# Loads at both ends of a four-layer graph network begun in another order, and single VectorE operations at the seams of layers 0 to 2 in another order

## The chip, the cores and the metric

One core of a Trainium2 chip runs the whole program in one launch. The time is device microseconds of that core, a median of three executions. The engines are TensorE (PE, with its weight loads as PEld), VectorE (DVE), ScalarE (ACT), GpSimd (POOL) and SyncE (SP), which issues nearly all DMAs.

## The reference

Everything is float32. There are 3327 nodes with 256 features; `adj` is a sparse symmetric 3327 x 3327 matrix with a full diagonal. Four layers are applied, each to a normalised and rectified copy of the nodes and added back to them:

```
h = relu(layernorm(x));  x = x + adj @ (h @ W0.T + b0)                                  # layer 0
h = relu(layernorm(x));  x = x + relu(new_adj @ (tanh(h @ Wp + bp) @ Wg) + bg)          # layer 1
      # new_adj = the 700 largest entries of each row of tanh(adj * adj), where adj > 0
h = relu(layernorm(x));  x = x + relu(dinv * (adj + I) @ (dinv * (h @ W2.T)))           # layer 2
h = relu(layernorm(x));                                                                # layer 3
   for n in 0, 1:
      A  = softmax(q k.T) cut to the entries that make 0.9 of each row, made to sum to 1
      Xf = R @ Xf;  Xa = A @ Xa;  Z += Xf @ U1[n].T + Xa @ U2[n].T
   x = x + layernorm(h + Z) * g + b
```

A row of `adj` has far fewer than 700 entries above zero, so in layer 1 the kernel counts the entries and keeps them all; code that would do it otherwise runs only if a count asks for it.

## The kernel before

The nodes make 26 tiles of 128 rows. Tile p and tile p + 13 form a pair p (13 pairs), so that `adj` falls into a 2 x 2 of 13 x 13 blocks, and a product with it is made by seven half-size products instead of eight (a scheme of Winograd's kind). For that, the blocks of the right-hand side are combined on VectorE (`combining_nodes`: L396 to L399, in chunks of blocks, into `ts`), and the slabs of `adj` too.

*Layers 0 to 2.* `Feed` brings the slabs: `load` (L565) issues the four slabs `a_a` of a chunk on SP (L576), `adding` (L594) makes the sums of them on VectorE (L608 to L611, in layer 2 after adding the identity on the diagonal blocks, L607), and `upto(n)` (L623) says which loads and sums are begun ahead of chunk n. A chunk is a stretch of the 13 blocks: in layer 0 (0 to 5, 5 to 9, 9 to 13), one pair at a time (`Product`, matmuls at L669); in layers 1 and 2 (0 to 3, 3 to 6, 6 to 9, 9 to 11, 11 to 13), two pairs at a time (`Double`, matmuls at L763). `count` (in `counter`, L868) notes the entries above zero of each slab (`pos`, L874 and L876); L891 takes the counts. `Double.result` (L773) takes the products out of PSUM: two copies on ScalarE, then five VectorE operations, L786 to L790. The doubles share one set of PSUM: products 1, 2, 5 and 4 of the next double need the copies out of the way, products 6, 3 and 7 (in TensorE's order 1, 2, 5, 4, 6, 3, 7) the operations up to L790.

*Layer 1* has a hidden product in front: for each pair, `hidden` (L499) adds a bias on VectorE (L504) and takes a tanh on ScalarE (L505), both on the 128 x 512 of tiles p and p + 13 of the right-hand side `rhs`. It runs in between the products of layer 0 that are still going on, and for the last pair, 12, at the start of layer 1. There the last two chunks of `ts` are combined inside `doubles` (L817, with the condition on `b`), after the third and the fourth `upto`.

*The order of the work.* TensorE's order is written out by hand everywhere. VectorE, SP and ScalarE follow the program's order only in `first_two_in`, the start of layer 0; elsewhere a scheduler orders them from the program's order, `tc.high_priority()` and `tc.issue_after(x)`, which puts what follows behind instruction x.

*The start.* `first_two` warms TensorE up with 15 matmuls of 128 x 128 of the identity (L958; float32, so two passes each), and 4 more behind the first `turn`. `first_two_in` (L963) issues on SP the nodes (L969, tile groups 0:1, 1:2, 2:4, 4:6, 6:9, 9:12, 12:13, each for both halves of the nodes) with the weights `w0s` (256 KB, L976) behind group 0:1. For each pair, `measure` takes mean and variance (L416, L417), `apply` normalises (L426, L433), `turn` transposes on TensorE (L445) with an eviction on ScalarE, and `plain` multiplies with `w0s` (L457).

*The end.* Layer 3's last two tiles, 25 and 12, come from the last `PropagatedPair`. After its second phase (slabs at L1414, products at L1539, `whole` with L1560 to L1566 on VectorE), `shares` loads rows of x3 and u (L1633, L1634), `finish3` and `finish_last` load z (L1642, L1675), all behind `pair.loaded`, the last slab's load. GpSimd adds u and y to z (L1644, L1645, L1676, L1677) and a bias to x3 (L1655, L1678), VectorE adds the product (L1647, L1684, L1686), makes a layer norm and adds x3 (to L1657 and L1692), and SP stores (L1665, L1693).

The lines that the change touches, and what calls them:

Of the kernel before, what the change touches and what calls it, by code (L numbers as in the profile page):

```python
# [16 lines left out]
AF = mybir.ActivationFunctionType  # L17
ALU = mybir.AluOpType
# [6 lines left out]
P = 128  # L25
# [31 lines left out]
def kernel(  # L57
# [255 lines left out]
    def layers_0_to_2(again):  # L313
# [123 lines left out]

        evicted, hold = [], []

# [23 lines left out]
        class Pair:  # L463
# [35 lines left out]
            def hidden(self):  # L499
                acc = project(self.xT, wps, self.name)  # L500
                rows = self.rhs.pair(self.p)
                by = bps.rearrange("p (i j f) -> p i j f", i=1, j=2).to_broadcast([P, 2, 2, P])
                with tc.high_priority():
                    nc.vector.tensor_tensor(rows, acc, by, ALU.add)  # L504
                    nc.scalar.activation(rows, rows, AF.Tanh)  # L505

# [48 lines left out]
        class Feed:  # L555
# [3 lines left out]
            def __init__(self, layer, order, load_x, change=None, count=None, keep=(), many=lambda p: 1):  # L559
                self.layer, self.order, self.load_x, self.many = layer, order, load_x, many  # L560
                self.change, self.count, self.keep, self.made = change, count, keep, []
                self.quads, self.ready, self.x2, self.done = {}, {}, {}, [0, 0]
                self.to_count = None

            def load(self, p, c):  # L565
# [8 lines left out]
                for i, j in QUADS:  # L574
# [9 lines left out]
                    q[i, j] = s  # L584
                if self.count:
                    if self.to_count is None:
                        self.count(p, c, q, many)
                    else:
                        self.to_count.append(functools.partial(self.count, p, c, q))
# [4 lines left out]
            def adding(self, p, c):  # L594
                many = self.many(p)
                a, b = cuts(many)[c]
                name = f"{tag}{self.layer}_{p}_{c}"
                q = self.quads.pop((p, c))
                s1, s2, s4 = (
                    raw.tile([P, 6, P], F32, tag=f"s{n}", name=f"s{n}_{name}", bufs=2)[:, : many * (b - a), :]  # L600
# [22 lines left out]
            def upto(self, n):  # L623
# [3 lines left out]
                if not n and self.layer:  # L627
                    turns = (self.load, 1), (self.add, 1), (self.load, 2), (self.add, 2), (self.load, 3)
                elif self.layer:
                    turns = (self.add, n + 2), (self.load, n + 3)  # L630
                else:
                    turns = (self.load, n + 3), (self.add, n + 2)
                for what, upto in turns:
                    k = what == self.add
                    while self.done[k] < min(upto, len(self.order)):
                        what(*self.order[self.done[k]])
                        self.done[k] += 1
                    if what == self.load:
                        self.store(n)
# [11 lines left out]
        class Product:  # L651
# [25 lines left out]
            def result(self, behind=None):  # L677
# [6 lines left out]
                with tc.high_priority():  # L684
# [10 lines left out]
                    nc.vector.tensor_tensor(four[:, 0, :], p1, p2, ALU.add)  # L695
                    nc.vector.tensor_tensor(four[:, 3, :], u[:, 0, :], b[:, 1, :], ALU.add)
                return y.rearrange("p i j f -> p i (j f)"), p3
# [36 lines left out]
        class Double:  # L734
# [36 lines left out]
            def result(self):  # L771
# [11 lines left out]
                with tc.high_priority():  # L783
# [5 lines left out]
                    nc.vector.tensor_tensor(y0[:, 1:2, :], y1[:, 1:2, :], one(3), ALU.add)  # L789
                    return nc.vector.tensor_tensor(y1, y1, both(one(7)), ALU.add)  # L790

# [11 lines left out]
        def doubles(layer, rhs, feed, w, finish, todo, at_first, places, pair_after, following=None, counted=None):  # L803
# [5 lines left out]
            for p in range(0, H, 2):  # L809
# [5 lines left out]
                for c, (a, b) in enumerate(cuts(prod.many)):  # L815
                    feed.upto(n)
                    if first and b > CUTS[2][0]:  # L817
                        combine_nodes(rhs, a, b)
                    for at in prod.steps(c, a, b):
# [5 lines left out]
                left = todo[len(places[prod.many - 1]) :] if p else []  # L825
                with tc.issue_after(prod.result().ins):
                    feed.upto(n)
# [91 lines left out]
        if not again:  # L919
# [33 lines left out]
            def first_two(product):  # L953
# [5 lines left out]

                warm_up(15)  # L960
                with tc.manual_schedule(engines=IN_FIRST_TWO):
                    return first_two_in(product, warm_up)

            def first_two_in(product, warm_up):
                for a, b in ((0, 1), (1, 2), (2, 4), (4, 6), (6, 9), (9, 12), (12, 13)):
                    for i in range(2):
# [5 lines left out]
                        else:  # L972
                            for r in LAST_ROWS:
                                nc.sync.dma_start(x0[r, a_, :], x[a_ * P + r.start : a_ * P + r.stop, :])
                    if a == 0:
                        nc.sync.dma_start(w0s, w0t.rearrange("(c p) e -> p c e", p=P))  # L976
# [22 lines left out]
                pairs[0].measure()  # L999
                for p in range(2):  # L1000
                    pairs[p + 1].measure()
                    pairs[p].apply()
                between = itertools.chain(add(), combining_nodes(rhs0, *CUTS[0]))
# [142 lines left out]
    def layer_3_in(again, tag, big, ep, w3, sm3, h3, kT0, ksum0, left):  # L1146
# [901 lines left out]
        with tc.manual_schedule(engines=PE_ALONE):  # L2048
# [31 lines left out]
            for i, m in enumerate(ORDER):  # L2080
# [34 lines left out]
                else:  # L2115
# [12 lines left out]
                    if not phase:  # L2128
                        pair.half()
                    else:  # L2130
                        both = pair.whole()
                        if pair.last:
                            with tc.issue_after(pair.loaded.ins):
                                x3s, us = shares(f"{p}", (1, m), (0, p))
                            finish3(m, ys.pop(m), both[:, 1, :], f"{m}", pair.loaded, (x3s[:, 1, :], us[:, 1, :]))()
                            finish_last(
                                p, ys.pop(p), both[:, 0, :], pair.accs[2][:, :P], f"{p}", pair.loaded,
                                x3s[:, 0, :], us[:, 0, :],
# [85 lines left out]
```

## Time and profile before

| what | value |
|---|---|
| median of 3 runs | 2466.09 us (2465.77 to 2466.48) |
| the profiled execution | 2464.7 us |
| its span, first to last instruction | 2462.9 us |
| mean granted TensorE clock | 0.998 |
| first matmul starts | 1.53 us |
| layer 1's first matmuls, layer 2's first matmuls | 329.99, 611.92 us |
| last matmul ends, last store issued, span ends | 2450.40, 2457.28, 2462.9 us |
| DVE busy in 320 to 365 us, 365 to 408, 705 to 750 | 44.09 of 45, 38.03 of 43, 29.02 of 45 us |

Two lists of the profile carry most of what follows. The list of waits says for how long an engine sat idle before an instruction of a line and which instruction ended that. The timeline gives for each group of like instructions the start, the duration, the engine, the line, and the tiles written and read, and in brackets the idle time just before. The matmuls overlap one another: their durations are longer than the distance between two, and a stall of the stream is better read from start to start.

### The profile page before, as it was taken

What the parts mean: (1) busy time and instruction counts of PE and PEld (TensorE: products, weight loads), DVE (VectorE), ACT (ScalarE), POOL (GpSimd) and SP (SyncE); (2) the same over time, 40 slices, a digit from 0 to 9 for tenths busy, and PEclk for the clock granted to TensorE, in tenths of its full rate; (3) what the DMA queues carried; (4) which work ended last, traced back from release to release, by engine and by line L of the source; (5) the groups of instructions that cost most, each with busy time, mean ns of one, the idle gap of its engine ahead of it and who ended that gap; (6) DMA issues with size and microseconds to landing.
All of it is one profiled execution on the core that took longest, in us unless ns stands there. A gap on an engine that the chain in (4) does not pass through costs nothing.

```text
span 2462.9 us, 41138 instructions
## 1 busy us (share of the span) xinstructions
PE 2443.5 (99%) x14483; PEld 2105.2 (85%) x14483; DVE 2078.8 (84%) x5312; ACT 1071.4 (44%) x2074; POOL 287.2 (12%) x462
## 2 busy tenths in 40 slices
PE   9999999999999999999999999999999999999997
PEld 8999988889888897777777777778888888888887
DVE  7877799898867768889788787995899999999995
ACT  3000034443011126666566565654655555555551
POOL 2000010000000000000000100000113222222232
PEclk9999999999999999999999999999999999999999
DMA  6788855566978666322332323234534434443343
GB/s 205 248 272 272 289 174 181 180 196 191 300 226 268 196 198 190 118 81 83 110 110 72 98 87 112 86 104 120 155 104 138 133 115 125 135 140 121 115 139 113
DMA packets 278674, 387.79 MB, mean 157 GB/s; under 512 B 24253, under 2 KB 216250, under 8 KB 278458
## 3 DMA queue, kind: packets, MB, share of 16 engines
q1 hardware_dynamic: 257322, 367.54, 48.3%
q10 hardware_dynamic: 21136, 17.52, 2.2%
q8 instruction: 116, 1.90, 0.3%
q14 instruction: 100, 0.82, 0.1%
HBM read 315.37 MB, written 67.89 MB: 156 GB/s over the span
## 4 chain that ended last, share of the span: by engine, by line
PE 94%; DVE 3%; DMA 1%; issue 1%; POOL 0%; SPq 0%; ACT 0%; POOLq 0%; DVEq 0%
PE a L234 24%; PE acc_a L763 18%; PE f0a L1480 11%; PE f1a L1539 10%; PE acc_a L669 10%; PE pl_a L1213 6%; PE pt_a L223 6%; PE u L1610 2%; PE u L1591 2%; PE out_a L797 2%; PE prj_a L457 2%; PE f L1381 1%; DVE a_a L906 1%; PE pt_a L445 1%; DMA a_a<-in_adj_t_dram 0%
## 5 line engine op out<-in xcount | busy, mean ns | idle before, releaser
L226 ACT COPY eT_a<-pt_a 128x512 f32<-128x512 f32 (+1 forms) x364 | 196.3, 554 | 372.0 <-PE pt_a L223 369.5
L234 PE MATMUL a<-h3a,eT_a 128*128 128x256 f32 x1352 | 320.3, 381 | 0.2 <-ACT eT_a L226 0.2
L234 PE MATMUL a<-vs,eT_a 128*128 128x256 f32 x1352 | 320.2, 381 | 0.2 <-ACT eT_a L226 0.2
L1300 DVE MAX8 cand_a<-w 128x8 f32<-128x128 f32 x1352 | 284.9, 278 | 4.1
L234 PEld LDWEIGHTS a<-h3a,eT_a 128*128 128x128 f32 x1352 | 246.5, 189 | 45.2 <-issue 10.0
L234 PEld LDWEIGHTS a<-vs,eT_a 128*128 128x128 f32 x1352 | 244.8, 190 | 30.3 <-ACT eT_a L226 0.7
L1296 DVE SCALAR_TENSOR_TENSOR w<-e_a,t_a 128x896 f32<-128x896 f32 x208 | 229.3, 1102 | 3.4
L1238 ACT ACTIVATE e_a<-pl_a 128x1024 f32<-128x1024 f32 x260 | 184.4, 728 | 36.7 <-PE pl_a L1213 36.7
L223 PE MATMUL pt_a<-ident,e_a 128*128 128x128 f32 x1352 | 198.3, 272 | 0.0
L1287 DVE SCALAR_TENSOR_TENSOR w<-e_a,t_a 128x3328 uint8<-128x3328 f32 x52 | 191.6, 3684 | 4.4
L223 PEld LDWEIGHTS pt_a<-ident,e_a 128*128 128x128 f32 x1352 | 166.5, 141 | 29.4
L1324 DVE SCALAR_TENSOR_TENSOR e_a<-e_a,all_least 128x3328 f32<-128x3328 f32 x50 | 184.5, 3690 | 1.8
L763 PE MATMUL acc_a<-s_a,tsa 128*128 128x256 f32 (+1 forms) x728 | 169.1, 364 | 2.7 <-DVE y_a L790 2.4
L763 PE MATMUL acc_a<-a_a,tsa 128*128 128x256 f32 (+1 forms) x728 | 169.4, 365 | 0.5 <-DVE tsa L399 0.5
L1480 PE MATMUL f0a<-slab3a_0a,tsa 128*128 128x256 f32 (+1 forms) x728 | 161.4, 367 | 0.0
L1271 ACT ACTIVATE junk_a<-e_a,t_a 128x3328 uint8<-128x3328 f32 x52 | 159.8, 3073 | 0.4
L763 PE MATMUL acc_a<-a_a,rhs 128*128 128x256 f32 (+1 forms) x728 | 158.6, 365 | 0.0
L908 ACT ACTIVATE a_a<-a_a 128x768 f32<-128x768 f32 (+2 forms) x132 | 97.3, 748 | 136.6 <-DVE a_a L906 98.2
L1276 ACT ACTIVATE junk_a<-e_a,t_a 128x3328 uint8<-128x3328 f32 x50 | 153.3, 3066 | 0.0
L1539 PE MATMUL f1a<-tsa,slab3a_1a 128*128 128x128 f32 x1248 | 148.1, 276 | 0.0
L763 PEld LDWEIGHTS acc_a<-s_a,tsa 128*128 128x128 f32 x728 | 130.5, 190 | 19.5 <-issue 2.5
L1539 PEld LDWEIGHTS f1a<-tsa,slab3a_1a 128*128 128x128 f32 x1248 | 144.0, 192 | 1.8
(284 smaller groups left out, 4316.9 us busy)
## 6 DMA issues: line engine op xcount, KB each, us to landing
a_a<-in_adj_t_dram SPq DMA_DIRECT2D x216, 256.0 KB, 3.4
a_a<-in_adj_t_dram SPq DMA_DIRECT2D x144, 384.0 KB, 4.1
slab3a_0a<-s_dram SPq DMA_DIRECT2D x95, 384.0 KB, 4.0
slab3a_0a<-in_adj_t_dram SPq DMA_DIRECT2D x65, 384.0 KB, 3.9
slab3a_1a<-s_dram SPq DMA_DIRECT2D x60, 384.0 KB, 4.0
a_a<-in_adj_t_dram SPq DMA_DIRECT2D x60, 320.0 KB, 4.4
slab3a_1a<-in_adj_t_dram SPq DMA_DIRECT2D x48, 384.0 KB, 4.0
s_dram<-s_a SPq DMA_DIRECT2D x45, 256.0 KB, 4.5
```

What stands on the lines that cost most here:

```text
L223: nc.tensor.transpose(pt[:, j, :], e[:, k * P : (k + 1) * P], ident)
L226: last_turned.append(nc.scalar.copy(eT[:, : len(blocks), :], pt[:, : len(blocks), :]))
L234: nc.tensor.matmul(acc[:, :width], ready[g][:, j, :], rhs[:, k, :], start=(k == 0), stop=(k == T - 1))
L669: nc.tensor.matmul(self.acc[:, g, at : at + wide], quads[n][:, k - CUTS[c][0], :], t, start=(k == 0 and n in (1, 4)), stop=(k == H - 1 and ...
L763: nc.tensor.matmul(self.acc[n], t, slab[:, :, k - cuts(self.many)[c][0], :], start=(k == 0 and n in (1, 5, 6, 7)), stop=(k == H - 1 and n ...
L1238: last_exp.append(nc.scalar.activation(dst, src, AF.Exp, accum_out=parts[:, c : c + 1]))
L1287: nc.vector.scalar_tensor_tensor(junk, e, t, e, ALU.is_lt, ALU.mult, accum_out=got)
L1296: nc.vector.scalar_tensor_tensor(w[:, : (b - a) * P], eg, t, eg, ALU.is_lt, ALU.mult, accum_out=below[:, g : g + 1])
L1300: nc.vector.max(cand[:, 8 * k : 8 * k + 8], w[:, (k - a) * P : (k - a + 1) * P])
L1324: nc.vector.scalar_tensor_tensor(e, e, least, e, ALU.is_ge, ALU.mult, accum_out=kept)
L1480: nc.tensor.matmul(self.acc[:, self.at[n]], right_half(h3, ts, n, k), self.block(phase, at), start=not at, stop=at == len(units) - 1, skip ...
L1539: nc.tensor.matmul(self.accs[bank][:, c * P : (c + 1) * P], self.block(phase, at)[:, 0, :], right_half(self.h, self.ts, n, k), start=start ...
```

## The change

- At the start, `w0s` is loaded behind the node tiles 2:4 instead of 0:1, and the first warm-up has 11 matmuls instead of 15. The loop around `measure` and `apply` is written out and gives the same order.
- In `hidden`, the last pair's bias and tanh are made in two halves (one for tile 12, one for tile 25).
- In `doubles`, the last two chunks of `ts` are combined one chunk earlier: blocks 9 to 11 before the products of chunk 2, blocks 11 to 13 before those of chunk 3.
- In layer 2 the counts of a chunk are made where its sums are made (`to_add`), and not where it is loaded. In layers 0 and 1 they stay.
- `summed_up` holds the last VectorE operation with which a product was taken out of PSUM (of `Product` or `Double`), and what follows a product is put behind it: at the start of layer 2 the loads and sums from the third of `turns` on; at the other doubles as before, by L790.
- At the end, `loaded` is kept from the last pair's first phase, so that the loads of x3, u and z stand behind the last slab of phase 0 instead of phase 1.

```diff
                         ALU.subtract, ALU.mult,
                     )
 
-        evicted, hold = [], []
+        evicted, hold, summed_up = [], [], []
 
         def turn_pair(src, func, pool, t, bufs, name):
 
...
                 rows = self.rhs.pair(self.p)
                 by = bps.rearrange("p (i j f) -> p i j f", i=1, j=2).to_broadcast([P, 2, 2, P])
                 with tc.high_priority():
-                    nc.vector.tensor_tensor(rows, acc, by, ALU.add)
-                    nc.scalar.activation(rows, rows, AF.Tanh)
+                    for i in (slice(0, 1), slice(1, 2)) if self.p == H - 1 else (slice(0, 2),):
+                        nc.vector.tensor_tensor(rows[:, i], acc[:, i], by[:, i], ALU.add)
+                        nc.scalar.activation(rows[:, i], rows[:, i], AF.Tanh)
 
             def hidden_turned(self):
                 acc = bank(f"hid_{self.name}")
...
                 self.layer, self.order, self.load_x, self.many = layer, order, load_x, many
                 self.change, self.count, self.keep, self.made = change, count, keep, []
                 self.quads, self.ready, self.x2, self.done = {}, {}, {}, [0, 0]
-                self.to_count = None
+                self.to_count, self.to_add = None, {}
 
             def load(self, p, c):
                 many = self.many(p)
...
                     if self.change:
                         self.change(s)
                     q[i, j] = s
-                if self.count:
+                if self.count and self.layer == 2:
+                    self.to_add[p, c] = functools.partial(self.count, p, c, q, many)
+                elif self.count:
                     if self.to_count is None:
                         self.count(p, c, q, many)
                     else:
...
                 a, b = cuts(many)[c]
                 name = f"{tag}{self.layer}_{p}_{c}"
                 q = self.quads.pop((p, c))
+                if (p, c) in self.to_add:
+                    self.to_add.pop((p, c))()
                 s1, s2, s4 = (
                     raw.tile([P, 6, P], F32, tag=f"s{n}", name=f"s{n}_{name}", bufs=2)[:, : many * (b - a), :]
                     for n in (1, 2, 4)
...
                 self.store(n - 1)
                 if not n and self.layer:
                     turns = (self.load, 1), (self.add, 1), (self.load, 2), (self.add, 2), (self.load, 3)
+                    for what, upto in turns[:2]:
+                        what(*self.order[0])
+                    self.done = [1, 1]
+                    with tc.issue_after(summed_up[-1].ins) if self.layer == 2 and summed_up else nullcontext():
+                        self.turns(n, turns[2:])
+                    return
                 elif self.layer:
                     turns = (self.add, n + 2), (self.load, n + 3)
                 else:
                     turns = (self.load, n + 3), (self.add, n + 2)
+                self.turns(n, turns)
+
+            def turns(self, n, turns):
                 for what, upto in turns:
                     k = what == self.add
                     while self.done[k] < min(upto, len(self.order)):
...
                     nc.vector.tensor_tensor(u[:, 0, :], u[:, 2, :], p5, ALU.add)
                     nc.vector.tensor_tensor(four[:, 1:3, :], u[:, :2, :], b[:, 2:4, :], ALU.add)
                     nc.vector.tensor_tensor(four[:, 0, :], p1, p2, ALU.add)
-                    nc.vector.tensor_tensor(four[:, 3, :], u[:, 0, :], b[:, 1, :], ALU.add)
+                    summed_up[:] = [nc.vector.tensor_tensor(four[:, 3, :], u[:, 0, :], b[:, 1, :], ALU.add)]
                 return y.rearrange("p i j f -> p i (j f)"), p3
 
 
...
                     nc.vector.tensor_tensor(y0[:, 1:2, :], y0[:, 1:2, :], one(6), ALU.add)
                     nc.vector.tensor_tensor(y1, y1, both(y0[:, 1:2, :]), ALU.add)
                     nc.vector.tensor_tensor(y0[:, 1:2, :], y1[:, 1:2, :], one(3), ALU.add)
-                    return nc.vector.tensor_tensor(y1, y1, both(one(7)), ALU.add)
+                    summed_up[:] = [nc.vector.tensor_tensor(y1, y1, both(one(7)), ALU.add)]
 
             def weighed(self, t):
 
...
                     hooks[88] = functools.partial(counted, p, prod.many)
                 for c, (a, b) in enumerate(cuts(prod.many)):
                     feed.upto(n)
-                    if first and b > CUTS[2][0]:
-                        combine_nodes(rhs, a, b)
+                    if first and c in (2, 3):
+                        combine_nodes(rhs, *CUTS_OF_DOUBLE[c + 1])
                     for at in prod.steps(c, a, b):
                         if at in hooks:
                             hooks[at]()
...
                     if prod.many == 1 and c and following:
                         combine_nodes(following, *CUTS[c - 1])
                 left = todo[len(places[prod.many - 1]) :] if p else []
-                with tc.issue_after(prod.result().ins):
+                prod.result()
+                with tc.issue_after(summed_up[-1].ins):
                     feed.upto(n)
                 pairs = []
 
...
                     for _ in range(n):
                         nc.tensor.matmul(busy[:, :P], ident, ident, start=True, stop=True)
 
-                warm_up(15)
+                warm_up(11)
                 with tc.manual_schedule(engines=IN_FIRST_TWO):
                     return first_two_in(product, warm_up)
 
...
                         else:
                             for r in LAST_ROWS:
                                 nc.sync.dma_start(x0[r, a_, :], x[a_ * P + r.start : a_ * P + r.stop, :])
-                    if a == 0:
+                    if a == 2:
                         nc.sync.dma_start(w0s, w0t.rearrange("(c p) e -> p c e", p=P))
                 feed.to_count = []
 
...
                     run(prods[p].steps(c, *CUTS[c]))
 
                 pairs[0].measure()
-                for p in range(2):
-                    pairs[p + 1].measure()
-                    pairs[p].apply()
+                pairs[1].measure()
+                pairs[0].apply()
+                pairs[2].measure()
+                pairs[1].apply()
                 between = itertools.chain(add(), combining_nodes(rhs0, *CUTS[0]))
                 for p in range(H):
                     pairs[p].turn()
...
                     run(pair.steps(phase), {k * units // T: v for k, v in plan.items()})
                     if not phase:
                         pair.half()
+                        loaded = pair.loaded
                     else:
                         both = pair.whole()
                         if pair.last:
-                            with tc.issue_after(pair.loaded.ins):
+                            with tc.issue_after(loaded.ins):
                                 x3s, us = shares(f"{p}", (1, m), (0, p))
-                            finish3(m, ys.pop(m), both[:, 1, :], f"{m}", pair.loaded, (x3s[:, 1, :], us[:, 1, :]))()
+                            finish3(m, ys.pop(m), both[:, 1, :], f"{m}", loaded, (x3s[:, 1, :], us[:, 1, :]))()
                             finish_last(
-                                p, ys.pop(p), both[:, 0, :], pair.accs[2][:, :P], f"{p}", pair.loaded,
+                                p, ys.pop(p), both[:, 0, :], pair.accs[2][:, :P], f"{p}", loaded,
                                 x3s[:, 0, :], us[:, 0, :],
                             )
                         else:
```

## The prediction

> **What bounds the kernel now.** I read the page's busy times and the summary of its chain of waits first: who sets the pace?
>
> ```profile
> PE 2443.5 (99%) x14483; PEld 2105.2 (85%) x14483; DVE 2078.8 (84%) x5312; ACT 1071.4 (44%) x2074; POOL 287.2 (12%) x462
> PE 94%; DVE 3%; DMA 1%; issue 1%; POOL 0%; SPq 0%; ACT 0%; POOLq 0%; DVEq 0%
> ```
>
> TensorE does, nearly alone. The change takes next to nothing from its stream, so it can only gain where that stream stands still, ahead of it, and behind it. The list of waits on TensorE says how much that is:
>
> ```profile
> PE acc_a L763 <- DVE y_a L790: 2.4, 2, 1.6
> PE busy L958 <- POOL ident masks.py:199: 1.5, 1, 1.5
> PE acc_a L763 <- ACT rhs L505: 1.0, 1, 1.0
> PE pt_a L445 <- DVE xn_a L433: 0.6, 2, 0.3
> PE acc_a L763 <- DVE tsa L399: 0.5, 1, 0.5
> ```
>
> Columns: total, times, longest. The first, third and fifth rows are the seams, and each lies on a line that the change touches. Then both ends, as the chain of waits gives them (start, length, what), first the beginning:
>
> ```profile
> 3.59 4.63 DMA rhs<-in_x_dram
> 8.24 0.44 DVE st_a L416
> 8.93 0.34 DVE xn_a L433
> 9.31 0.75 PE pt_a L445 x4
> 10.10 1.99 PE prj_a L457 x8
> ```
>
> The program waits for the seventh load (rows 2 to 4, second half, landed 8.22), normalises the first tile of pair 1 behind it, and transposes; from 10.10 on TensorE runs. And the end, VectorE's timeline around the idle time that GpSimd ends:
>
> ```profile
> 2448.57 0.42 DVE L1566 TENSOR_TENSOR xf_1a<-xf_1a,f1a 128x256 f32<-128x256 f32 x1
> 2452.41 0.48 DVE L1684 SCALAR_TENSOR_TENSOR z<-xf_1a,rinv,z 128x256 f32<-128x256 f32 x1 [3.42 <-POOL z L1677]
> ...
> 2453.95 0.32 DVE L1686 SCALAR_TENSOR_TENSOR z<-f1a,rinv,z 128x128 f32<-128x128 f32 x1
> ```
>
> **The start.** In SP's order `w0s` leaves third place for seventh; no other load changes its order. Each 2-tile load and `w0s` carry 256 KB. Of the chain's two last loads, the first landed at 7.48 and the second at 8.22, one such load apart. With `w0s` no longer ahead of them I take each to land one load earlier, the second at 7.48, and `w0s` at 8.22. The rest follows: VectorE's statistics, normalising and transpose take 8.24 to 10.10 as before, less 0.74; the product with `w0s` could start at 9.36, 1.1 after `w0s`. Gain 0.74. Bounds: by SP's issue alone the load moves by one issue (0.43 + 0.04 in the chain) = 0.47; by the spacing of the two loads before (6.25 to 7.48), 1.23. If instead `w0s` slipped a place further, to 9.59 where the (4:6) load landed, the product would start near 9.65: 0.45. VectorE's loads (4:6), at 8.86 and 9.59, are past `w0s` anyway and keep their place. Warm-up: eight passes fewer. Its matmuls stand 0.213 us apart until 5.53 and 0.112 after (the clock rises 4.0 us after the first), so it ends 8 x 0.112 = 0.9 before its 7.09, at 6.2, still 0.67 behind the rise; and the first transpose follows at once: at 7.34 before, it waited for an input that stood on VectorE behind the statistics of pair 1 (landed 6.25), whose load now lands by about 4.9, so that its input is there by 6.2. So it costs nothing; if the clock did not rise in time, the price is a window at half rate.
>
> A rule stands against this cut. The Trainium skill, "TensorE: Matmul & The Clock Gate", section "Part 1: The HAM clock gate (the "warmup" mystery)", has the clock released after a busy window of about 3.4 us that runs freely, so that the rise can fall later in another execution. By it another 3.4 us at half rate would lose an estimated 1.7 us, and the sum below would be some 7 instead of 8.7; the trace has only the one rise, at 5.53, and I go by that.
>
> **Layer 0 to 1.** Two stalls. At 357.39 TensorE waits for the tanh L505 (until 358.42) though it reads only blocks 19 to 21: the write goes over tiles 12 to 25 at once. In halves the ranges no longer touch, so this wait falls away. At 363.87 it waits for L399 of blocks 9 to 11, which now stand right behind the halves, ahead of most of the sums, and are done at about 359.6 (two halves from 356.96, 0.35 each, then L396 to L399 at 0.33 and one sum of 0.6), where TensorE needs them near 362.3. From start to start the stream lost 358.42 - 355.93 - 1.295 = 1.20 and 364.39 - 362.85 - 0.864 = 0.68 (1.295 and 0.864 being the usual six- and four-matmul groups): **1.88**. By idle time the two are 1.04 + 0.52. What is late next: VectorE issues one more operation pair (0.1 us) and TensorE is then 1.9 ahead of it; the sums of 9 to 11 come at about 363.1 with TensorE there at 364.0, and L790 at about 376.2 with the need near 377.5. VectorE is busy 38 of 43 us in layer 1, so it catches up. Lower bound: all but the first wait reappears, 1.2.
>
> **Layer 1 to 2.** L790 ends at 618.00 because two `pos` operations stand ahead of it; it releases 618.15. They go behind it, two `ts` operations (0.33 each) come between. It then ends at 617.03, and TensorE, issuing from 615.81 + 1.295 = 617.10, waits at most 0.1. From start to start: 618.15 - 617.10 = 1.05, less 0.01 to 0.1: **1.04**.
>
> **First seam inside layer 2.** VectorE idles until 747.39 for a slab (landed 747.37) that `pos` counts, and L786 to L790 (751.33 + 0.69) stand behind it; TensorE waits until 752.16. Their inputs are there at 745.4, so ahead of `pos` they end at about 746.8. Gain 752.16 - 749.15 - 1.295 = **1.72**. What goes behind: two `pos` per chunk, 2 x 0.87 = 1.74 (six by 0.69 to 0.96 in the rows of L876), now before the sums. The smallest slack of a sum's first use after 660 us was 7.5 (I took each use's start less the end of its writer); the sum of this seam comes earlier than before, at 749.6 instead of 751.93. Counts are used 14 us late. So moving them costs nothing at 7.5 of slack and starts to cost at 1.74. At the other doubles there was no stall, and no gain.
>
> **The end.** Six loads of 128 KB were issued from 2443.21 on, because they stood behind the last slab, whose buffer came free at 2442.84. They landed to 2449.71, GpSimd's four additions and two more followed one another (0.72 each) to 2452.38, and L1684 waited 3.42. Behind the last slab of the first phase they go out at about 2424 to 2430, between the slabs of the second phase. GpSimd is done by about 2442.8 (the last addition needs the attention product of 2441.47). On SP they put six issues of 0.43 us ahead of slabs, and in the DMA engines 768 KB (2.6 us at the 300 GB/s moved there): 2.6 against the 8 us between the landing of these slabs, by 2433, and their first use at 2441.3. L1684 then needs only its place behind L1563, 2448.57. L1566 at 2448.99, L1647 2449.45, L1649 2449.96, L1685 2450.30, L1651 2450.50, and L1686 at 2450.58 instead of 2453.95, where the last matmul (end 2450.40, plus 0.13) becomes the other limit. Gain **3.37**; bounds 2.5 (a wait at the last addition or slab of 0.9) and 3.5. The tail behind L1686 stays.
>
> **Sum.** 0.74 + 1.88 + 1.04 + 1.72 + 3.37 = 8.75, or 8.1 with the idle rows (4.0) for the seams; I take 8.7. The profiled span of 2462.9 (time 2464.7, 1.8 around it) becomes 2454.2 and its time 2456.0. The median of runs is 1.4 above that execution: 2466.09 - 8.7 = **2457.4**.
>
> **Rivals.**
>
> 1. *The seams form again.* VectorE was busy 44.09 of 45 us at 320 to 365; the stalls were its lateness, and would be due again one product further on (margins worked out above: 0.1, 0.9, 1.3). For it: those margins; against: only two halves of an operation are added, the rest is order. Only both ends gain: 2466.09 - 0.74 - 3.37 = 2462.0, no change within what can be told.
> 2. *The start gives nothing or loses.* `w0s` and the loads around it share the DMA engines and land together, late, or the clock rises late. Seams and end: 8.01 less nothing to 1.7: 2458.1 to 2459.8.
> 3. *Slower: counts in the way.* Two `pos` ahead of the sums on VectorE, 30 chunks in six doubles of layer 2. It decides when the slack of a sum falls under 1.74: at 0.87, say, 30 x 0.87 = 26.1 are lost and the time is 2466.09 - 8.7 + 26.1 = 2483.5. For it: the sums come later at every chunk. Against: 7.5 us, and VectorE is busy 29 of 45 us there.
> 4. *The change does not do what it says*: VectorE's scheduler undoes an order. The order of instructions shows each move as told, so it is left with 0.03 and 2466.
>
> **How the numbers follow.** Forecast 0.67, rival 1 0.11, rival 2 0.14, rival 3 0.05, rival 4 0.03. The forecast's own range is 2455.7 (start 1.23, end 3.5: a gain of 9.4, and 1 us for the scatter of medians) to 2459.1 (start 0.47, seams 4.0, end 2.5: 7.0). To hold eight in ten I add rival 2 and the half-formed cases of rival 1 (half of the seams: 2466.09 - 0.74 - 2.3 - 3.37 = 2459.7, with the lower bounds about 2461): 2455.3 to 2461.0. A measurement tells about 0.2%, 4.9 us, from no change. Faster by more: forecast, rival 2 = 0.81, with a piece of rival 1 0.82; within: 0.12; slower: 0.06 (rival 3 and small losses).
>
> **What would show it.** The list of waits without L790, L505 and L399 over 0.2; the second transpose at 8.6 and the first product at 9.4; the clock's rise still near 5.5; L1684 1.8 before the last matmul's end and not 2.0 after it, with no idle time that GpSimd ends; and the last store 3.5 after the last matmul instead of 6.9. Wrong would be: a new row of waits for s_a or a_a in L763 in layer 2, or slabs at L1539 waiting for DMA behind the six loads.

## The result and the profile after

| | before | after |
|---|---|---|
| median, 15 runs each | 2465.49 us (2463.41 to 2467.11) | 2459.62 us (2458.61 to 2461.90) |
| profiled span | 2462.9 us | 2458.1 us |
| last matmul ends | 2450.40 us | 2448.55 us |
| last matmul's end to the span's end | 12.5 us | 9.5 us |

The ratio is 0.9976 with a 95% interval of 0.9969 to 0.9983: 5.9 us faster (4.2 to 7.6 by the interval), where 8.7 had been forecast. The list of TensorE's waits in the changed kernel (who waited for whom: total us, times, longest us; the lines have moved, L790 is now L804, L785 L799, L696 L710, L505 L506):

```profile
PE acc_a L777 <- ACT y_a L799: 2.4, 3, 1.7
PE acc_a L777 <- DVE y_a L710: 1.9, 1, 1.9
PE busy L973 <- POOL ident masks.py:199: 1.5, 1, 1.5
PE pt_a L445 <- DVE xn_a L433: 1.0, 1, 1.0
```

The three rows that the prediction wanted gone are gone: nothing waits for L804, for the tanh or for L399. But two rows stand in their place that it did not have: 2.4 us for the copies L799 on ScalarE, and 1.9 us for L710, the last operation that takes layer 0's last product out (0.2 before). They add up to 4.3 us; the seams' waits had been 4.0. So the stalls were exchanged, not removed? The start of the same matmul in the two traces tells how much of each gain lasted (after less before):

| matmul near (after) | 300 | 336 | 358 | 363 | 374 | 461 | 547 | 618 | 751 | last ends |
|---|---|---|---|---|---|---|---|---|---|---|
| difference, us | -1.00 | +0.63 | -0.57 | -1.35 | +0.41 | +1.05 | +1.32 | +0.28 | -1.46 | -1.84 |

The start brings 1.00, lost again at 336. The first seam brings 2.0 between 336 and 363, and 374 takes 1.8 of it. Two more stalls follow in layer 1. Behind 547 us come the steps at 618 (1.04) and 751 (1.74), and 0.4 in small ones. The one at 751 is no gain of the change, as the last part of this section and e11 show.

The places of the two losses, as the timeline has them (start, length, engine, line, what; in brackets the idle time before and who ended it). Layer 0's end, first VectorE, then TensorE:

```profile
332.68 0.95 DVE L616 TENSOR_TENSOR s_a<-a_a,s_a 128x768 f32<-128x768 f32 x1
...
334.56 0.95 DVE L921 SCALAR_TENSOR_TENSOR a_a<-a_a 128x768 f32<-128x768 f32 x1
335.43 0.41 DVE L708 TENSOR_TENSOR y_a<-u_a,acc_a 128x256 f32<-128x256 f32 x1
335.76 0.28 DVE L710 TENSOR_TENSOR y_a<-u_a,acc_a 128x128 f32<-128x128 f32 x1
```

```profile
332.88 1.46 PE L777 MATMUL acc_a<-a_a,tsa 128*128 128x256 f32 x6
336.19 1.10 PE L777 MATMUL acc_a<-s_a,tsa 128*128 128x256 f32 x4 [1.85 <-DVE y_a L710]
```

VectorE has sums and filters of layer 1 ahead of L708 and L710, and no gap. TensorE came 1.0 earlier than before, VectorE 0.63 later: it had waited until 305.66 for a slab that it counts (304.92 before). The end of the first double in layer 1, ScalarE and then TensorE:

```profile
372.55 0.84 ACT L923 ACTIVATE a_a<-a_a 128x768 f32<-128x768 f32 x1 [1.76 <-DVE a_a L921]
373.29 1.05 ACT L799 COPY y_a<-acc_a 128x512 f32<-128x512 f32 x2
```

```profile
371.67 1.03 PE L777 MATMUL acc_a<-a_a,tsa 128*128 128x256 f32 x4
374.40 0.92 PE L777 MATMUL acc_a<-a_a,rhs 128*128 128x256 f32 x3 [1.71 <-ACT y_a L799]
```

ScalarE sits idle for 1.76 us for a filter of VectorE's (L921), because the tanh L923 of a slab that is used later stands ahead of the copies in its queue. The kernel before had the same order there (the tanh at 371.85, the copies from 372.60 on), but TensorE needed the copies no earlier than they came. TensorE's next double may not write that PSUM until the copies are done.

The seams further on. VectorE ahead of 750 us in the changed kernel:

```profile
747.63 0.29 DVE L612 TENSOR_TENSOR a_a<-a_a,ident 128x128 f32<-128x128 f32 x1 [1.49 <-DMA a_a<-in_adj_t_dram]
747.84 0.69 DVE L802 TENSOR_TENSOR y_a<-y_a,y_a 128x512 f32<-128x512 f32 x1
...
749.09 0.69 DVE L804 TENSOR_TENSOR y_a<-y_a,acc_a 128x512 f32<-128x512 f32 x1
749.69 0.95 DVE L891 SCALAR_TENSOR_TENSOR pos<-a_a,pos 128x768 bf16<-128x768 f32 x1
```

The counts are behind L804 now, but the addition of the identity, L612, is still ahead of it, and it waits for a slab of its own: that one landed at 747.60, the slab that the counts wait for at 745.15. So L804 ends at 749.8, in time, and not at 746.8. The kernel before has the same addition (L607 there) in the same place, and its slab landed at 749.78:

```profile
749.87 0.28 DVE L607 TENSOR_TENSOR a_a<-a_a,ident 128x128 f32<-128x128 f32 x1
...
751.33 0.69 DVE L790 TENSOR_TENSOR y_a<-y_a,acc_a 128x512 f32<-128x512 f32 x1
```

From the start of this addition to the end of the last sum it takes 2.14 to 2.15 us in both, and in every one of the fourteen profiles of this study, whether the counts are ahead or behind. Without the counts ahead of it, L790 would therefore have ended near 751.9 by this estimate, and it ended at 752.01.

And both ends. First TensorE at the beginning, then VectorE at the end:

```profile
8.31 0.75 PE L445 MATMUL pt_a<-ident,xn_a 128*128 128x128 f32 x4 [0.97 <-DVE xn_a L433]
9.13 1.97 PE L457 MATMUL prj_a<-w0s,xT_a 128*128 128x256 f32 x8
```

```profile
2446.79 0.48 DVE L1700 SCALAR_TENSOR_TENSOR z<-xf_1a,rinv,z 128x256 f32<-128x256 f32 x1
2447.20 0.41 DVE L1582 TENSOR_TENSOR xf_1a<-xf_1a,f1a 128x256 f32<-128x256 f32 x1
...
2448.85 0.32 DVE L1702 SCALAR_TENSOR_TENSOR z<-f1a,rinv,z 128x128 f32<-128x128 f32 x1
```

The first product starts 0.97 earlier. L1700 is ahead of the last matmul's end (2448.55) by 1.8, as foretold, and L1702 is 0.30 behind it, where it was 3.55.

### The profile page after: what moved, and what is told of

The parts are those of the page before. It is cut to its first block, busy times and chain, and to the rows that moved or that the text cites. A ratio compares the mean times of both kernels' runs of the same rounds, so it can differ in the third digit from the quotient of the medians.

```text
span 2458.1 us, 41131 instructions
## 1 busy us (share of the span) xinstructions
PE 2441.2 (99%) x14475; PEld 2103.9 (86%) x14475; DVE 2078.7 (85%) x5313; ACT 1070.9 (44%) x2075; POOL 292.9 (12%) x462
## 5 line engine op out<-in xcount | busy, mean ns | idle before, releaser
L923 ACT ACTIVATE a_a<-a_a 128x768 f32<-128x768 f32 (+2 forms) x132 | 97.4, 748 | 139.8 <-DVE a_a L921 98.0
L777 PEld LDWEIGHTS acc_a<-a_a,rhs 128*128 128x128 f32 x728 | 129.8, 190 | 19.4 <-ACT y_a L799 3.9
```

What stands on the lines that cost most here:

```text
L777: nc.tensor.matmul(self.acc[n], t, slab[:, :, k - cuts(self.many)[c][0], :], start=(k == 0 and n in (1, 5, 6, 7)), stop=(k == H - 1 and n ...
```

## The experiments

Every ratio below is to the kernel before, run on the same chip; the interval is 95%.

| run | median us (runs) | before | ratio (interval) |
|---|---|---|---|
| e1 changed kernel again | 2459.98 (10) | 2466.16 (32) | 0.9976 (0.9966 to 0.9985) |
| e2 start alone | 2464.73 (11) | 2466.16 | 0.9997 (0.9988 to 1.0006) |
| e3 end alone | 2463.44 (11) | 2466.16 | 0.9988 (0.9979 to 0.9997) |
| e4 seams alone | 2463.38 (11) | 2466.16 | 0.9991 (0.9982 to 1.0000) |
| e5 copies first | 2457.45 (5) | 2465.35 (15) | 0.9964 (0.9950 to 0.9978) |
| e6 fewer counts | 2457.24 (5) | 2465.35 | 0.9965 (0.9952 to 0.9979) |
| e7 slabs behind L710 | 2462.34 (11) | 2465.35 | 0.9988 (0.9978 to 0.9997) |
| e8 first seam undone | 2460.60 (11) | 2465.21 (17) | 0.9979 (0.9970 to 0.9988) |
| e9 e5, first seam undone | 2458.28 (7) | 2465.21 | 0.9970 (0.9959 to 0.9981) |
| e10 e5, late count | 2455.98 (5) | 2465.21 | 0.9961 (0.9947 to 0.9974) |

**e1, the changed kernel again.** No edit.

> The changed kernel once more, to see whether the two new waits come back. Theory A (VectorE works without a break from about 306 to 376 us, and the copies L799 on ScalarE stand behind a tanh that waits for it, so what TensorE wins ahead of 374 us is lost there again): waits on L710 near 1.9 us in all and on L799 near 2.4, 5 to 6 us faster than before. Rival B (one slab landed late by chance in that one profile): the wait on L710 at most 0.5 us, and the time 7 to 9 us faster than before.

L799 2.2 us in all, 1.7 of it at 373 us; L710 1.1. The wait on the copies belongs to the kernel. That on L710 came back smaller, between the two theories: part of it varies. There is also a wait of 0.5 us on L804, near 796 us: VectorE stood idle for 3.68 us until the slab of L612 had landed (792.96), and four of the five operations that take the product out stood behind it.

**e2, the start alone**, on the kernel before:

```diff
-                warm_up(15)
+                warm_up(11)
...
-                    if a == 0:
+                    if a == 2:
                         nc.sync.dma_start(w0s, w0t.rearrange("(c p) e -> p c e", p=P))
```

> Only the start of the change (w0s later, 11 warm-up matmuls) on the kernel before. Theory A: TensorE's first product starts 1.0 us earlier, but this is lost as a longer wait on L696 near 335 us (0.23 before, 0.8 to 1.2 then), so 0 to 0.4 us of gain in the time. Rival B: nothing takes it back, 0.9 to 1.0 us of gain.

The first product starts at 9.10, and at 335 us TensorE waits 0.79 for L696, about what theory A said; but other profiles with the old order have 0.2 to 1.3 there, so this one wait does not decide. The median is 1.4 us lower, but the interval has no change in it, so the time does not decide either. Nothing waits for L790 at 750 us in this profile.

**e3, the end alone**, on the kernel before:

```diff
                     if not phase:
                         pair.half()
+                        loaded = pair.loaded
...
-                            with tc.issue_after(pair.loaded.ins):
+                            with tc.issue_after(loaded.ins):
                                 x3s, us = shares(f"{p}", (1, m), (0, p))
```

and `loaded` for `pair.loaded` in the two calls that follow.

> Only the end of the change (x3, u and z loaded behind phase 0's last slab). Both theories: nothing before 2420 us moves; from the last matmul to the end 9.5 us instead of 12.5, so 3.0 us of gain. If it were 3.4, as forecast, the 0.3 us more that the last store took in the profile after would be chance.

2.7 us by the medians, and 10.1 us from the last matmul to the end in the profile. Over all profiles of this study that stretch is 12.1 to 13.1 us in the five with the old end (mean 12.5) and 9.4 to 10.1 in the nine with the new (mean 9.7): 2.8 us.

**e4, the seams alone**: the changed kernel with the edits of e2 and e3 undone, so

```diff
-                warm_up(11)
+                warm_up(15)
...
-                            with tc.issue_after(loaded.ins):
+                            with tc.issue_after(pair.loaded.ins):
```

> Only the order at the seams of layers 0 to 2, with start and end as before. Theory A: the waits on L505 and L399 go and come back as a wait of 1.4 to 1.8 us on the copies L799 near 373 us; what stays is the gain at 617 and 750 us, 2.6 to 3.2 us in all. Rival B: 4.2 to 4.7 us, with no new wait in layer 1 over 0.3 us.

2.8 us by the medians, 1.7 us of wait on L799, 1.6 on L710: as theory A had it, and not 4.6. That the sum agrees is partly luck: theory A counts 1.6 us at 750, which e11 and e12 show to be no gain, and the interval reaches from no change to 4.4 us. With the start as before, L710 is waited for 1.6 us all the same.

**e5, the copies first.** On the changed kernel; the tanh of the last two slabs of a double's second chunk waits for its place behind the copies:

```diff
-                        self.change(s)
+                        self.change(s, late=p and c == 1 and i)
...
                     for y, b in zip(self.ys, self.banks):
-                        nc.scalar.copy(y, b.rearrange("p (n f) -> p n f", n=2))
+                        copied = nc.scalar.copy(y, b.rearrange("p (n f) -> p n f", n=2))
+                with tc.issue_after(copied.ins):
+                    while late_tanhs:
+                        late = late_tanhs.pop(0)
+                        nc.scalar.activation(late, late, AF.Tanh)
...
+            if late:
+                late_tanhs.append(a)
+                return
             with tc.issue_after(evicted[-1].ins) if evicted else nullcontext():
                 nc.scalar.activation(a, a, AF.Tanh)
```

> The changed kernel, with one more order: in layer 1 the tanh of the last two slabs of each double's second chunk is begun behind the two copies L799 on ScalarE, not ahead of them. Theory A1 (what takes TensorE's gain back at 373 us and at the later ends of doubles is this place in ScalarE's queue): no wait on L799 over 0.3 us in layer 1, nothing in its place, so 1.5 to 2.5 us faster than the changed kernel (7.5 to 8.5 faster than before). Rival A2 (VectorE as a whole is late there, and the copies only show it): the wait comes back a few products later on L804 or on a sum, 0 to 0.7 us faster than the changed kernel.

ScalarE at the same place, and TensorE's list of waits, in e5:

```profile
370.63 0.84 ACT L931 ACTIVATE a_a<-a_a 128x768 f32<-128x768 f32 x1 [1.11 <-DVE a_a L926]
371.38 1.05 ACT L799 COPY y_a<-acc_a 128x512 f32<-128x512 f32 x2
373.15 0.84 ACT L803 ACTIVATE a_a<-a_a 128x768 f32<-128x768 f32 x1 [0.71 <-ACT y_a L799]
```

```profile
PE acc_a L777 <- DVE y_a L710: 2.0, 1, 2.0
PE busy L981 <- POOL ident masks.py:199: 1.5, 1, 1.5
```

The copies start right behind the matmuls that they read, the next double follows without a stall, and no other wait appears in layer 1. From the matmul near 336 us, which L710 releases, to the one near 374 it takes 36.34 us here and 38.21 in the changed kernel. The time is 7.9 us below the kernel before, as theory A1 had it: it was the place in ScalarE's queue. By the medians that is 1.7 to 2.0 us below the changed kernel, less than the intervals are wide, but four of the five runs lie below all 25 of the changed kernel (2457.91 at the least).

**e6, fewer counts.** The last pair is not counted in layer 0:

```diff
             def count(p, c, q, many=1):
+                if not i and p == H - 1:
+                    return
...
                 m = p + i * H
+                if not i and p == H - 1:
+                    nc.gpsimd.memset(counts[:, m : m + 1], 0.0)
+                    return
```

> The changed kernel without the counting of the last pair in layer 0 (left out: the nine counting operations of that pair on VectorE, about 5 us of its work near 290 to 309 us, and its column of counts is set to zero). Theory A (VectorE, busy without a break from 306 to 376 us, is late, and starts that stretch when a slab that it counts has landed): the wait on L710 falls below 0.3 us and the one on L799 at 373 us below 0.5, 2 to 3.5 us faster than the changed kernel. Rival B (the waits come from landings that do not depend on VectorE): both stay over 1 us.

```profile
PE acc_a L777 <- ACT y_a L799: 2.0, 4, 1.5
PE busy L978 <- POOL ident masks.py:199: 1.5, 1, 1.5
```

The wait on L710 is gone from the list: that one is VectorE's lateness. Without the counts VectorE has both less to do and one slab less to wait for; this run does not part the two. The copies are still waited for, 1.5 at 371 us: this half of theory A's expectation failed, since both engines came earlier and the order in the queue stayed. Time as much below before (8.1 us) as e5.

**e7, slabs behind L710.** On the changed kernel:

```diff
-                    with tc.issue_after(summed_up[-1].ins) if self.layer == 2 and summed_up else nullcontext():
+                    with tc.issue_after(summed_up[-1].ins) if summed_up else nullcontext():
```

> The changed kernel with layer 1's second chunk, loads, filters and sums, put behind the last operation that takes layer 0's last product out (L710): three filters of 0.87 us leave VectorE's queue ahead of L710, and four operations of the last blocks of ts (0.33 each) come in. Theory A (VectorE's amount of work, not its order, sets this stretch): the wait on L710 goes, but one of 1 to 2 us comes at the sums or filters of the second chunk near 341 us, and the time is within 1 us of the changed kernel or slower. Rival (order alone): no wait in its place, 1.1 to 1.9 us faster than the changed kernel.

```profile
PE acc_a L777 <- DVE s_a L613: 3.3, 1, 3.3
PE busy L973 <- POOL ident masks.py:199: 1.5, 1, 1.5
PE acc_a L777 <- ACT y_a L799: 1.0, 1, 1.0
```

L710 is off the list, and a wait of 3.3 us on the second chunk's sum is on it, ending at 343.6 us. VectorE's order only chooses what is late in this stretch. By the medians it is some 3 us slower than the changed kernel. The wait is longer than the 1 to 2 us that were expected, and in this profile the idle time also throttled the clock (last section).

**e8 and e9, the first seam undone**, in the changed kernel and in e5:

```diff
-                    for i in (slice(0, 1), slice(1, 2)) if self.p == H - 1 else (slice(0, 2),):
-                        nc.vector.tensor_tensor(rows[:, i], acc[:, i], by[:, i], ALU.add)
-                        nc.scalar.activation(rows[:, i], rows[:, i], AF.Tanh)
+                    nc.vector.tensor_tensor(rows, acc, by, ALU.add)
+                    nc.scalar.activation(rows, rows, AF.Tanh)
...
-                    if first and c in (2, 3):
-                        combine_nodes(rhs, *CUTS_OF_DOUBLE[c + 1])
+                    if first and b > CUTS[2][0]:
+                        combine_nodes(rhs, a, b)
```

> The changed kernel with the first seam as before: the last pair's bias and tanh in one piece, and the last two chunks of ts combined one chunk later. Theory A (TensorE's gain at this seam only waits longer for ScalarE's copies at 373 us): waits of 1.0 us on the tanh and 0.5 on L399 come back, the one of 1.7 us on the copies at 373 us falls below 0.3, and the time is within 0.7 us of the changed kernel. Rival (the gain of 1.9 us forecast for this seam is there): 1.5 to 2.0 us slower than the changed kernel.

> The kernel of e5 (copies ahead of the late tanhs), with the first seam as before, as in e8. Theory A: with the copies out of the way, the seam is worth what its waits were, so this one is 1.2 to 2.0 us slower than e5. Rival (VectorE's lateness takes the gain in any case): within 0.5 us of e5.

In both, the waits on the tanh (1.0) and on L399 (0.5) come back, and in e8 none is left at 373 us: the longest on the copies is now 0.9, at 548. By the medians below their own before, e8 stands at 4.6 us where the changed kernel has 5.9 to 6.2, and e9 at 6.9 where e5 has 7.9. By these the seam is worth 1.3 to 1.6 us in the changed kernel and 1.0 in e5, between the theories both times; but each of these differences is smaller than the intervals are wide. The traces say more. From the matmul near 336 us (released by L696 or L710) to the one near 374 it takes 38.43 us in all seven profiles with the first seam as before (before, e2, e3, e8, e9, e11, e12), 38.21 in the three with the new seam and ScalarE's queue as it was (after, e1, e4), and 36.34 and 36.27 with the copies first (e5, e10). Up to 374 us the seam is then worth 0.2 us in the changed kernel and 2.1 with the copies out of the way, close to theory A both times. What the medians show beyond that is not explained by this seam.

**e10, the copies first and a late count.** On e5, the last pair's upper half is counted in layer 2, where these slabs pass again:

```diff
+            def count2(p, c, q, many=1):
+                count2_(p, c, q, many)
+                if p == H - 1:
+                    count0(p, c, q, many)
```

with layer 0 leaving this pair out, and the counts of pairs 10 and 11 taken 16 steps earlier (`hooks[72 if p == 10 else 88]`), so that their tile comes free.

> The kernel of e5, with the counting of the last pair's upper half moved from layer 0 to layer 2, where that pair's slabs pass again (nothing is left out). Theory A: the wait on L710 near 335 us falls below 0.3, as in e6; 1.5 to 2.5 us faster than e5, less what eight more counting operations cost at the end of layer 2 (0 to 1.5 us as a wait on y near 905 us). Rival: VectorE's work at the end of layer 2 costs all of it, same as e5 or slower.

```profile
PE busy L989 <- POOL ident masks.py:199: 1.5, 1, 1.5
PE pt_a L445 <- DVE h3a L489: 1.0, 1, 1.0
PE pt_a L445 <- DVE xn_a L433: 0.5, 1, 0.5
```

Behind the start no wait over 0.1 us is left in layers 0 and 1; one of 1.0 came near 897 us, not on y but on a node tile that VectorE makes for layer 3. 9.2 us below before, and its five runs (2455.49 to 2457.17) lie below all 25 of the changed kernel (2457.91 at the least). By the medians it is the fastest kernel of this study, 1.3 to 1.5 us ahead of e5, where theory A less its costs had 0 to 2.5; the intervals of the two overlap.

**e11 and e12, the kernel before twice more**, for its waits (one run each, 2465.14 and 2467.00 us). No edit.

> The kernel before once more, unchanged, for its waits alone. Theory (the wait of 1.6 us on L790 at 750 us was one late landing, and so no part of what the change can gain): no wait over 0.2 us near 750 us, as in e2 and e3, which have the old order there; the one of 0.9 near 617 us is there again; near 335 us 0.2 to 0.8 us on L696. Rival (it belongs to the old order): 1.2 to 1.6 us near 750 us again.

> The same a third time, with the same expectations as e11; of the waits on the copies L785 at the ends of layer 1's doubles, between none and 3 us in all, as landings fall.

Two rows of e11's list:

```profile
PE acc_a L763 <- ACT y_a L785: 1.2, 2, 1.0
...
PE acc_a L763 <- DVE y_a L790: 0.9, 1, 0.9
```

In all four further profiles with the old order (e2, e3, e11, e12) the wait on L790 is 0.9 us, once, near 618 to 622; the 1.6 near 750 us is in none (0.05 at most). It is a race: in e11 the slab of L607 landed at 749.74, as late as in the first profile (749.78), but TensorE came there 2.4 us later and did not wait. The copies, absent from the list of the first profile, are waited for 0.4, 3.1, 1.2 and 1.9 us. And L696: 0.8, 0.5, 1.3, 1.3, against 0.2.

## Why the prediction was right, and where not

**The time** lay in the stated range, but the gain was only two thirds of the 8.7: less than the forecast's own range (7.0 to 9.4), and nearest to the half-formed case of rival 1 (2459.7, a gain of 6.4). There is luck in it: of the five terms, 1.7 us of the first seam came back as another wait, and the 1.72 at 750 us was no gain of the change.

**The start.** Forecast 0.74 at the first product; it was 0.97 between the two first profiles, and over all of them 10.1 to 10.6 us became 8.3 to 9.1 (means 10.27 of five, 8.81 of nine): 1.46. The mechanism was right and the term too small: 0.97 lies within its bounds, the mean beyond the upper one of 1.23. That it stays with the program was not shown: e2's interval includes no change, and its profile loses half of its 1.00 to L696 at 335 us. What releases TensorE there is tied to the count of one slab (next paragraph), which began at 305.8 us in the mean of the five profiles with the old start and at 305.2 in that of seven with the new one. Against 1.46 at the first product this is 0.6, within a scatter from 304.2 to 306.6: most of the start's gain is likely waited for at that place.

**Layer 0 to 1.** Here a step failed: "What is late next". It compared VectorE's sums and L790 with TensorE's need and found 0.9 and 1.3 us to spare. It left out that the next double also needs the copies on ScalarE, and that these stand behind a tanh whose input VectorE makes late. That queue gave up 1.7 of the 1.9 us ten microseconds on (waits of 1.71, 1.71 and 1.70 us in the first profile, e1 and e4), so that 0.2 of the 1.88 stayed. At later doubles it costs up to 0.7 us in these three, but 0 to 3.1 with the old order too. e5 shows the cause by taking it away. Rival 1 named the right weakness (VectorE's lateness) and the wrong engine for its place. And L696, 0.2 us in the profile at hand and so left alone, is 0.2 to 1.3 in five profiles with the old order and 1.1 to 2.0 in six with the new one (0 in e6, e7, e10). How late VectorE is there was decided by the count that begins when a slab has landed, at 304.2 to 306.6 us: L696 or L710 ends 30.4 to 30.6 us later in ten profiles of both orders (31.1 in e12, where another slab was late; e6 and e10 do not count it, and e7 has another order). Up to that count VectorE and SP have the same order in e4 as in the kernel before, so the order at the seams does not make these waits longer. With the old start the new order has 1.6 in e4, where that count began last of all, at 306.60; with the new start TensorE is there earlier and the slab hardly so.

**Layer 1 to 2.** Right, in place and size: 1.04 forecast, 1.04 measured, and the 0.9 us wait is in every profile with the old order. L804 ends at 618.25 and not at 617.03, because VectorE and TensorE were both 1.3 us later there.

**The seam inside layer 2.** Forecast 1.72, and the profile after shows 1.74: but the agreement is luck, and this was no gain of the change. No other profile of the old order has the stall. Two steps failed. A single wait for DMA was read as a fixed cost. And "ahead of `pos` they end at about 746.8" left out the addition of the identity (L607, now L612), which stands among these sums and waits for a slab of its own, landed at 749.78: with that slab, moving the counts would have freed L790 some 0.1 us earlier, by the 2.15 us that follow this addition in every profile. It kept its place, so such a stall can return, as in e1 near 796 us. Moving the counts cost nothing, as said: no wait for a sum in layer 2 appears, and rival 3 found no case.

**The end.** Mis-sized: 3.37 against 2.8 over all profiles (2.7 in e3's time). L1702 did come nearer to the last matmul: 0.30 us behind its end in all nine with the new end, where it was 3.07 to 3.96 (mean 3.49) in the five with the old, a gain of 3.2. But from VectorE's last operation to the end of the program it takes 5.84 to 6.47 us in the nine (mean 6.1) and 5.65 to 5.83 in the five (mean 5.7). The working took this tail as fixed; it took back 0.4, and why stays open.

What the traces show as kept is 0.2 (first seam) + 1.0 (618) + 2.8 (end): 4.0 of the measured 5.9 to 6.2. The rest, some 2 us, is not settled: what the start keeps (0 to 1.46) and the copies at the later doubles, which wait 0 to 3.1 us from one execution to the next, can both have a part in it. The three parts alone gave 1.4 + 2.8 + 2.7 = 6.9 by their medians, the whole 6.2 on the same chip.

## What to carry to other kernels

A wait that a single profile shows for a DMA's landing is one draw. Profile the old kernel a few times before counting it as something to win, and see what else stands between the instruction to be freed and its inputs. When a stall is removed, look for the next one in every engine's queue and not only in the one that was late: what counts is what stands ahead of the instruction in its own queue, and what that in turn waits for. And where an engine is busy for tens of microseconds on end (VectorE 57.8 of the 59 us from 317 to 376 here), changing its order picks the victim; moving work out of the stretch, as in e10, removes the wait.

## What the runs showed of the hardware

The clock's rise at the start was taken as fixed at 5.53 us. The granted clock in the profile does not show it (it reads 1.00 over the first 5.5 us, before and after), but the distance between the warm-up matmuls does. It halved at anything from 4.5 to 6.2 us in thirteen profiles (4.5 in the changed kernel's first, 6.2 in e9), and in e8 only near 7.5, behind the 11 matmuls. The Trainium skill, "TensorE: Matmul & The Clock Gate", section "Part 1: The HAM clock gate (the "warmup" mystery)", says that the window runs freely, which agrees with this; the spread that it gives, 500 ns to either side, is smaller than the 3 us of these profiles. It cost nothing measurable here, since the first product waits for loads: 9.13 in e8 too.

The same section has the clock throttled again after an idle window of about 3.4 us. In e7 TensorE idled for 3.26 us, and the windows around it (us; busy time and instructions of PE, PEld, DVE, ACT, POOL; the granted clock; DMA share and GB/s) read:

```profile
336.00:340.00 4.00, 4.00 (x21) 3.48 (x19) 3.09 (x9) 1.69 (x2) 2.85 (x3) 1.00 0.21 70
343.60:346.80 3.20, 3.19 (x8) 2.57 (x9) 3.20 (x4) 0.84 (x1) 0.00 (x0) 0.51 0.00 0
347.00:351.00 4.00, 4.00 (x22) 3.54 (x21) 4.00 (x7) 2.27 (x4) 0.00 (x0) 1.00 0.63 193
```

For 3.2 us the clock was granted at 0.51, eight matmuls went through instead of about 15, and some 1.6 us were lost beyond the wait. So a stall of 3.3 us was enough here, a little less than the page's figure, and the price of one slow window is about the 1.7 us that the prediction had estimated for the start. Behind the other stalls of layers 0 to 2, 2.0 us at the longest, the granted clock stayed at 1.00.
